# One keys' pass per chunk in the additive attention, and another order of work at the end of the last layer

## The chip, the cores and the metric

The kernel runs on one core of a Trainium2 chip. The core's engines are TensorE (PE in the profile; its weight loads stand apart as PEld), VectorE (DVE), ScalarE (ACT), GpSimd (POOL) and SyncE (SP). Here SP issues nearly all of the DMA transfers. Each engine works through its own queue in order, and waits on semaphores for the others. "granted clock" (PEclk) is the share of TensorE's full clock that it was granted in a stretch.

The metric is the device time of one execution in microseconds. The kernel before was run three times: 6970.31, 6976.12 and 6979.77, median 6976.12.

## The reference

Four layers work on four images (B = 4) of 56 x 56 tokens with 128 channels, in float32. Only layers 2 and 3 are touched. With `t` of shape (4, 3136, 128) they compute:

```python
# layer 2: additive attention (16 hidden units), then an expert layer
xn = layernorm(t)
f, g = xn @ W1[:128], xn @ W1[128:]                   # (4, 3136, 16): queries and keys
s = einsum('bija,a->bij', tanh(f[:, :, None] + g[:, None] + b1), w2) + b2
e = exp(s) * strictly_lower_triangle
t = t + (e / (e.sum(-1) + 1e-10)) @ xn
p = softmax(layernorm(t) @ gate_w.T, axis=tokens)     # 64 experts, each takes its 8 tokens
t = t + scatter(experts(gather(p)), p)                # 128 -> 512 -> 128, gelu
# layer 3: attention of the tokens on themselves, then a mixture of 8 experts
xn = layernorm(t)
t = t + softmax(xn @ xn.T) @ xn
xn = layernorm(t)
gate = two largest of softmax(xn @ router_w), divided by their sum
t = t + sum over e of gate[:, e] * (xn @ expert_w[e] + expert_b[e])
```

The `tanh` of layer 2 is the large term: for each pair of a query and an earlier key there are 16 of them.

## The kernel before, in words

All of `t` stays on the chip in `X[b]`, as 28 tiles of 112 tokens an image, each [112 tokens, 128 channels]. The time of the span goes to layer 0 until about 500, to layer 1 (a state-space scan) until about 2985, to layer 2 until about 5552 and to layer 3 until 6972.4.

**Layer 2's attention** (`layer2_attention`, L1139). An image has four chunks of seven query tiles (WT = 7, 784 queries), 16 chunks in all. A chunk goes over its key tiles J, from the image's first to the chunk's own last, and each key tile in two halves; (chunk, key tile, half) is a *piece*, and `pieces` lists all of them in order. One piece goes through five steps on three engines:

- `adds` (VectorE, L1298): seven operations that add one column of the keys' term `g` to the queries' term `fT` [128, up to 784], written into one of three rooms `th` of a ring;
- `tangents` (ScalarE, L1307): one Tanh over the whole room, in place;
- `scores` (TensorE, L1321): 28 small matmuls by `place`, which holds w2, into the bank `s`;
- `weights` (ScalarE, L1335): Exp once both halves are there; in the chunk's own key tiles GpSimd masks one square (L1342);
- `weighted` (TensorE, L1351): matmuls of `e` with the normalised tokens `xk` into `o`.

The piece loop issues, for piece i, in this order: the tanh of i, the *first slot* (`deal`), the adds of i + 2, at the first half of a key tile the `weighted` of an earlier key tile, the scores of i, what the first slot left for VectorE, the Exp of an earlier piece, and the *second slot* (`deal`). The order on each engine is the order of this text (a manual schedule). A slot takes one step from four lists: `urgent`, `now`, `later_on` (in every other slot) and `behind`. Narrow pieces, those at the diagonal, have fewer slots: a slot costs credit, which a piece gives in proportion to its width. A step may return a function, its VectorE part; the part of a first slot runs behind the scores of the same piece, that of a second slot at the start of the next slot. So a first slot's matmuls stand before the adds and scores, a second slot's behind them.

**A chunk's preparation** (`chunk_steps`, L1208) is such a list of steps, made for the first four tiles and then for the other three: `norm` twice (VectorE, two tiles each, into `xa`, L1222), `turn` (TensorE turns the tiles, L1231, VectorE copies the bank into `xT`, L1234), `by_group` (GpSimd sets the ones column at L1238, SP issues eight DMAs that carry `xa` to `xk` in another order of rows), `keys` (eight matmuls over 56 or 42 columns, L1254, then VectorE's add of `b1` into `g`, L1262) and `queries` (one matmul over 448 or 336 columns, L1272, then VectorE's copy into `fT`, L1276). That makes twelve steps. `xa` and `xT` each have one room, of four tiles, and the PSUM bank `m`, through which `turn`, `keys` and `queries` pass, is a single one too. The steps of an image's next chunk come at key tile 1 of the chunk before. Those of the next image's first chunk come at key tile 8 of the image's last one, through `later_on`, behind fifteen steps of statistics (`image_steps`) that end with a square root on ScalarE (`root`, by way of `rstd`, L175, with its scratch `li_ve` and `li_q`). When the loop comes to the first adds of a new chunk and steps are left in `now` or `later_on`, `add_ahead` runs all of them in one go, called the drain below. The first chunk of all has its own code (`first_chunk`, L1374).

What comes behind the attention of an image, the choice of 8 tokens for each of 64 experts (`choose_steps`, L1596), its experts and the scatter of their results (`experts2_steps`, scatter matmuls at L1822), are steps of `behind`. The choice has a second square root, by `rstd` with the scratch `ln_ve` and `ln_q`. Whatever is left in `behind` at the end of layer 2 runs there, but for the last 14 steps (`carried`), which are dealt into the first units of layer 3.

**Layer 3** has units (image, chunk of four tiles, key tile of 128): seven chunks (0 to 6) and 25 key tiles, `weights` (one matmul, one Exp) and `weighted` (one matmul) each. When a chunk's last `o` matmul (L2005) is behind it, its steps are dealt to the following units by their numbers: `copied` (VectorE and ScalarE copy `o` to `oT`, L1969 and L1970), `added` twice (L1539 to L1547), then `normed_chunk` (statistics, root, newton, norm, turn) and `token_choice` (L2147): router, `choose` (the gates, L2184 to L2194), `experts` and `store`. `experts(k)` takes one tile through two matmuls (four experts each, L2200, into two rooms `pe`) and eight operations of VectorE that multiply an expert's product by its gate and add it to X (L2205). These stand at

```python
    + [(21 + 2 * k, bind(experts, k)) for k in range(TC)] + [(21 + 2 * TC, store)]
```

that is, with the 4 that `experts_chunk` adds, at least 25 units behind the chunk's end. For the last two chunks of the last image there are no units left there, and their steps run one after the other in order of number.

Of the kernel before, what the change touches and what calls it, by code (L numbers as in the profile page):

```python
# [11 lines left out]
AF = mybir.ActivationFunctionType  # L12
# [126 lines left out]
class Hybrid:  # L139
# [35 lines left out]
    def rstd(self, pool, var, shape, eps, tag, bufs=None):  # L175

        nc = self.nc
        ve = self.t(pool, shape, tag + "_ve", bufs=bufs)
# [4 lines left out]
        q = self.t(pool, shape, tag + "_q", bufs=bufs)  # L183
# [955 lines left out]
    def layer2_attention(self):  # L1139
# [5 lines left out]
        with ExitStack() as ctx:  # L1145
# [62 lines left out]
            def chunk_steps(j):  # L1208
# [18 lines left out]
                def turn(at, w):  # L1227
                    r["xT"] = self.t(big, [P, CH], "xT")
                    ps = m()
                    for i in range(w):  # L1230
                        nc.tensor.transpose(  # L1231
                            ps[:, i * TP : (i + 1) * TP], r["xa"][:, i, :], self.ident[:TP, :TP]
                        )
                    return lambda: nc.vector.tensor_copy(r["xT"][:, : w * TP], ps[:, : w * TP])  # L1234
# [15 lines left out]
                def keys(at, w):  # L1250
                    ps = m()[:, : w * NG]
                    by_key = r["xT"][:, : w * TP].rearrange("p (g j) -> p g j", j=JG)
# [6 lines left out]
                    def keyed():  # L1259
                        if at == 0:  # L1260
                            g[b, k] = self.t(big, [P, WT * NG], f"g{k}")
                        nc.vector.tensor_scalar(  # L1262
                            g[b, k][:, at * NG : (at + w) * NG], ps, b1, None, op0=ALU.add
                        )
# [3 lines left out]
                def queries(at, w):  # L1268
                    if at == 0:
# [3 lines left out]
                        ps, wf.rearrange("p j a -> p (j a)"), r["xT"][:, : w * TP],  # L1273
# [4 lines left out]
                for at in range(0, n, TC):  # L1278
                    w = min(TC, n - at)
                    steps += [bind(norm, at, 0, 2), bind(norm, at, 2, w)]  # L1280
                    steps += [bind(f, at, w) for f in (turn, by_group, keys, queries)]
                return steps
# [91 lines left out]
            def first_chunk():  # L1374
# [5 lines left out]
                xT = [self.t(big, [P, CH], "xT"), self.t(sm, [P, WT * TP], "fT")]  # L1380
# [470 lines left out]
    def layer3(self):  # L1851
# [6 lines left out]
        with ExitStack() as ctx:  # L1858
# [103 lines left out]
            def experts_chunk(b, c):  # L1962
# [9 lines left out]
                def added(s):  # L1972
# [5 lines left out]
                    + [(k + 4, f) for k, f in self.token_choice(b, c, w, sm, m, ps_e)]  # L1978
# [168 lines left out]
    def token_choice(self, b, c, w, sm, m, ps_e):  # L2147
# [62 lines left out]
        def store():  # L2210
            dst = self.out[b].rearrange("h w c -> (h w) c").rearrange("(t p) c -> p t c", p=TP)
            nc.sync.dma_start(out=dst[:, TC * c : TC * (c + 1), :], in_=x4)

        bind = lambda f, *args: lambda: f(*args)
        return (
            self.normed_chunk(b, c, sm, m, w["eps"], turned, ones=True)
            + [(10, route), (12, exp), (13, choose)]
            + [(21 + 2 * k, bind(experts, k)) for k in range(TC)] + [(21 + 2 * TC, store)]
        )

# [47 lines left out]
```

## Time and profile before

| what | us |
|---|---|
| median of three runs | 6976.12 |
| the profiled execution: its time | 6974.18 |
| the profiled execution: its span | 6972.4 |
| mean granted clock of TensorE | 0.935 |
| busy in the span: PE / DVE / ACT / POOL | 6051.8 / 5757.1 / 4834.7 / 2787.6 |
| Tanh of layer 2 (L1307), 559 records | 2177.6, idle before it 138.4 |
| adds of layer 2 (L1298), 3920 records | 1864.2, idle before it 232.7 |
| scores of layer 2 (L1321), 14112 records | 1387.5 |
| experts of layer 3 on VectorE (L2205), 896 records | 311.8, idle before it 306.7 |

The profiled execution lies 1.94 below the median. In a row of the groups, the time after the bar is the busy time of the group and the mean duration of one in ns; after the second bar stands how long the engine stood still just before these instructions, and what ended most of that. A row of the waits reads "who waited <- for whom: us, times" and, where there is a third number, the longest. A row of the timeline has the start, the duration and the instruction, and in square brackets the wait ahead of it. A row of the windows has the stretch, its length, the busy time of PE, PEld, DVE, ACT and POOL with the number of instructions, the granted clock, and the DMA engines' share and rate.

### The profile page before, as it was taken

The numbers are of one execution on the slowest core, as the hardware profiler recorded it, in microseconds if no ns is written. First come the engines' busy times: TensorE is split into PE (matmuls) and PEld (weight loads), VectorE is DVE, ScalarE is ACT, GpSimd is POOL, SyncE is SP. The second block draws the span as 40 slices with busy tenths as digits, with TensorE's granted clock in tenths as the row PEclk, the third lists the DMA queues.
The fourth block names the chain that finished last, engine by engine and source line by source line (L and its number), as shares of the span: only waits on it lengthen the run. The fifth ranks groups of instructions, "written<-read, shape, count | busy, mean of one in ns | idle before, by whom it ended". The sixth has DMA issues, their size and how long they took to land.

```text
span 6972.4 us, 103013 instructions
## 1 busy us (share of the span) xinstructions
PE 6051.8 (87%) x37386; PEld 2623.8 (38%) x37386; DVE 5757.1 (83%) x10104; ACT 4834.7 (69%) x4839; POOL 2787.6 (40%) x1921
## 2 busy tenths in 40 slices
PE   8889989998999999877777877877788799999998
PEld 7633332333233333232233323332333355555554
DVE  6879999999999999988878888888897753566665
ACT  5567667766766677679999998999899833322231
POOL 2369989998999999910000000100101100000000
PEclk9989989998999899889998999999899999999999
DMA  3057767776777677700000000000003204343433
GB/s 53 5 138 189 184 162 186 186 182 169 187 184 179 174 187 184 178 9 3 1 6 3 8 2 6 4 6 3 6 20 123 83 21 149 78 108 89 119 86 95
DMA packets 363457, 654.29 MB, mean 94 GB/s; under 512 B 95412, under 2 KB 211908, under 8 KB 362437
## 3 DMA queue, kind: packets, MB, share of 16 engines
q1 hardware_dynamic: 362949, 647.71, 37.0%
q8 instruction: 296, 4.85, 0.3%
q14 instruction: 212, 1.74, 0.1%
HBM read 536.78 MB, written 104.37 MB: 92 GB/s over the span
## 4 chain that ended last, share of the span: by engine, by line
PE 23%; ACT 11%; DVE 11%; issue 10%; POOL 1%; SPq 1%; DMA 1%; DVEq 0%; ACTq 0%; POOLq 0%
ACT th L1307 9%; PE o L2005 6%; DVE th L1298 6%; PE q L1993 5%; PE s L1321 4%; PE pe L2200 2%; DVE X L2205 2%; ACT e L1335 1%; PE o L1351 1%; DVE wide L2025 1%; PE m L1254 1%; PE m L1539 1%; PE m L1822 0%; POOL e L1342 0%; DVE X L1547 0%
## 5 line engine op out<-in xcount | busy, mean ns | idle before, releaser
L1307 ACT ACTIVATE th<-th 128x5488 f32<-128x5488 f32 (+13 forms) x559 | 2177.6, 3944 | 138.4 <-DVE th L1298 124.2
L1298 DVE TENSOR_SCALAR th<-fT,g 128x784 f32<-128x784 f32 (+13 forms) x3920 | 1864.2, 548 | 232.7 <-PE s L1321 221.0
L1321 PE MATMUL s<-th,place 128*32 128x392 f32 (+5 forms) x14112 | 1387.5, 487 | 456.1 <-ACT th L1307 454.1
L860 DVE TENSOR_TENSOR_SCAN hs<-E,u 128x896 f32<-128x896 f32 x728 | 1449.1, 2006 | 3.9 <-ACT E L844 3.9
L844 ACT ACTIVATE E<-E,rate 128x448 f32<-128x448 f32 x1456 | 885.8, 661 | 127.2 <-DMA E<-delta_dram 124.3
L865 POOL TENSOR_TENSOR hs<-hs,room 128x896 f32<-128x896 f32 x448 | 925.5, 2087 | 82.6 <-DVE hs L860 82.2
L1321 PEld LDWEIGHTS s<-th,place 128*32 128x32 f32 (+1 forms) x14112 | 456.9, 112 | 1323.3 <-ACT th L1307 687.4
L865 POOL TENSOR_TENSOR hs<-hs,bc 128x896 f32<-128x896 f32 x448 | 927.3, 2090 | 46.7 <-DVE hs L860 44.1
L1998 ACT ACTIVATE e<-q,shift 128x448 f32<-128x448 f32 (+1 forms) x511 | 322.5, 634 | 669.3 <-PE q L1993 650.3
L1342 POOL TENSOR_TENSOR e<-e,later 112x112 f32<-112x112 f32 x112 | 102.3, 914 | 1178.3 <-ACT e L1335 670.8
L2205 DVE SCALAR_TENSOR_TENSOR X<-pe,r_gate,X 112x128 f32<-112x128 f32 x896 | 311.8, 348 | 306.7 <-PE pe L2200 271.1
L871 PE MATMUL y<-hs,sum 128*32 128x448 f32 x3584 | 499.4, 631 | 4.0 <-POOL hs L865 4.0
L1993 PE MATMUL q<-xT 128*128 128x448 f32 (+1 forms) x1022 | 499.5, 571 | 0.9 <-ACT e L1998 0.9
L2005 PE MATMUL o<-e,xk 128*128 128x448 f32 (+1 forms) x1022 | 477.6, 551 | 16.0 <-ACT oT L1970 16.0
L806 PE MATMUL u<-room,pick 32*128 32x448 f32 x1456 | 413.6, 638 | 68.5 <-DVE hs L860 66.6
L806 PE MATMUL u<-du,pick 32*128 32x448 f32 x1456 | 402.8, 618 | 74.3 <-DVE hs L860 72.9
L1351 PE MATMUL o<-e,xk 112*128 112x392 f32 (+5 forms) x1024 | 393.9, 505 | 34.6 <-POOL e L1342 31.5
L1238 POOL MEMSET xa<- 112x4 f32 (+1 forms) x30 | 55.0, 1832 | 919.6 <-PE m L1231 919.6
L853 DVE TENSOR_TENSOR u<-u,bc 128x896 f32<-128x896 f32 x364 | 391.8, 1077 | 25.9 <-PE u L806 25.7
L853 DVE TENSOR_TENSOR u<-u,room 128x896 f32<-128x896 f32 x364 | 391.7, 1076 | 22.0 <-PE u L806 21.9
L2134 POOL MEMSET lc_xa<- 112x4 f32 x28 | 3.1, 110 | 943.5 <-DVE lc_xa L2128 694.6
L848 ACT ACTIVATE u<-u 128x896 f32<-128x896 f32 x168 | 151.9, 904 | 296.9 <-PE u L797 217.2
(333 smaller groups left out, 8768.1 us busy)
## 6 DMA issues: line engine op xcount, KB each, us to landing
E<-delta_dram SPq DMA_DIRECT2D x728, 448.0 KB
V<-du_dram SPq DMA_DIRECT2D x168, 448.0 KB
wide<-in_L_ffn_weight SPq DMA_DIRECT2D x64, 1024.0 KB
r<-M SPq DMA_DIRECT2D x189, 224.0 KB
M<-wide SPq DMA_DIRECT2D x72, 392.0 KB
du_dram<-room SPq DMA_DIRECT2D x112, 112.0 KB
delta_dram<-room SPq DMA_DIRECT2D x112, 112.0 KB
du_dram<-du SPq DMA_DIRECT2D x112, 112.0 KB
```

What stands on the lines that cost most here:

```text
L806: nc.tensor.matmul(halves(to)[:, k], w["pick"][own, q, :], pre[j]["du"][own, f], start=True, stop=True,)
L844: nc.scalar.activation(e, e, AF.Exp, scale=rate)
L853: eng.tensor_mul(v, v, pre[p // PAIRS]["bc"][:, 0:1].to_broadcast([P, 2, CH]))
L860: nc.vector.tensor_tensor_scan(flat, E.pop(p), V.pop(p), 0.0, op0=ALU.mult, op1=ALU.add)
L865: nc.gpsimd.tensor_mul(HS[p], HS[p], bc[:, 1:2].to_broadcast([P, 2, CH]))
L871: nc.tensor.matmul(py[j, f][r * HD : (r + 1) * HD, :], w["sum"][:, q, :], HS[p + r // 2][:, r % 2], start=False, stop=(q == QG - 1),)
L1298: nc.vector.tensor_scalar(th[i][:, s, lo:hi], fT[j][:, lo:hi], g[b, J // WT][:, at : at + 1], None, op0=ALU.add,)
L1307: nc.scalar.activation(own, own, AF.Tanh)
L1321: nc.tensor.matmul(ps[j, J][QW * blk : QW * blk + rows, h, lo:hi], place[:, off : off + rows], z[:, at + s, h * HALF + lo : h * HALF + hi] ...
L1351: nc.tensor.matmul(po[j][:, h, lo:hi], xk[b, J // WT][:, J % WT, :], e[:, h * HALF + lo : h * HALF + hi], start=(J == 0), stop=(J == t + ( ...
L1993: nc.tensor.matmul(ps[:n, :CH], of_tile(xT[b], t), xT[b][:, c * CH : (c + 1) * CH], start=True, stop=True,)
L2005: nc.tensor.matmul(po[b, c], xk[b][:n, t, :], e[:n], start=first, stop=last)
```

## The change

In `chunk_steps`, `xT` holds seven tiles in place of four. Each `turn` writes its own part of it and `queries` reads its own part. `keys` is one step for the whole chunk, eight matmuls over 98 columns and one add, and stands before the last `queries`; the preparation has eleven steps. `first_chunk` takes its `xT` in the new size. The two square roots of layer 2 share the names, and so the rooms, of their scratch (`rt_ve`, `rt_q`).

In layer 3, the last chunk but one of the last image has its expert steps at 15, 16, 17 and 18. The last chunk has one step, `last_experts`: tiles 0 and 1 by `experts`, and between them tiles 2 and 3 another way. Their matmuls go into banks of `m` and of `q`, ScalarE multiplies the eight products of a tile by the gates into a room `y`, and VectorE sums the eight with one reduction and adds the sum to X. The chunk is stored in two halves.

```diff
@@ -175,12 +175,12 @@
     def rstd(self, pool, var, shape, eps, tag, bufs=None):
 
         nc = self.nc
-        ve = self.t(pool, shape, tag + "_ve", bufs=bufs)
+        ve = self.t(pool, shape, "rt_ve", bufs=bufs)
         nc.vector.tensor_scalar(ve, var, eps, None, op0=ALU.add)
         r = self.t(pool, shape, tag + "_r", bufs=bufs)
         nc.scalar.activation(r, ve, AF.Sqrt)
         nc.vector.reciprocal(r, r)
-        q = self.t(pool, shape, tag + "_q", bufs=bufs)
+        q = self.t(pool, shape, "rt_q", bufs=bufs)
         nc.vector.tensor_mul(q, r, r)
         nc.vector.tensor_mul(q, q, ve)
         nc.vector.tensor_scalar(q, q, -0.5, 1.5, op0=ALU.mult, op1=ALU.add)
@@ -1225,13 +1225,15 @@
                         )
 
                 def turn(at, w):
-                    r["xT"] = self.t(big, [P, CH], "xT")
+                    if at == 0:
+                        r["xT"] = self.t(big, [P, WT * TP], "xT")
+                    own = r["xT"][:, at * TP : (at + w) * TP]
                     ps = m()
                     for i in range(w):
                         nc.tensor.transpose(
                             ps[:, i * TP : (i + 1) * TP], r["xa"][:, i, :], self.ident[:TP, :TP]
                         )
-                    return lambda: nc.vector.tensor_copy(r["xT"][:, : w * TP], ps[:, : w * TP])
+                    return lambda: nc.vector.tensor_copy(own, ps[:, : w * TP])
 
 
                 def by_group(at, w):
@@ -1247,9 +1249,9 @@
                                 in_=r["xa"][of : of + rows, :w],
                             )
 
-                def keys(at, w):
-                    ps = m()[:, : w * NG]
-                    by_key = r["xT"][:, : w * TP].rearrange("p (g j) -> p g j", j=JG)
+                def keys():
+                    ps = m()[:, : n * NG]
+                    by_key = r["xT"][:, : n * TP].rearrange("p (g j) -> p g j", j=JG)
                     for i in range(JG):
                         nc.tensor.matmul(
                             ps, wg[:, P - AH - i * AH : 2 * P - AH - i * AH], by_key[:, :, i],
@@ -1257,11 +1259,8 @@
                         )
 
                     def keyed():
-                        if at == 0:
-                            g[b, k] = self.t(big, [P, WT * NG], f"g{k}")
-                        nc.vector.tensor_scalar(
-                            g[b, k][:, at * NG : (at + w) * NG], ps, b1, None, op0=ALU.add
-                        )
+                        g[b, k] = self.t(big, [P, WT * NG], f"g{k}")
+                        nc.vector.tensor_scalar(g[b, k][:, : n * NG], ps, b1, None, op0=ALU.add)
 
                     return keyed
 
@@ -1270,7 +1269,7 @@
                         fT[j] = self.t(sm, [P, WT * TP], "fT")
                     ps = m()[:, : w * TP]
                     nc.tensor.matmul(
-                        ps, wf.rearrange("p j a -> p (j a)"), r["xT"][:, : w * TP],
+                        ps, wf.rearrange("p j a -> p (j a)"), r["xT"][:, at * TP : (at + w) * TP],
                         start=True, stop=True,
                     )
                     return lambda: nc.vector.tensor_copy(fT[j][:, at * TP : (at + w) * TP], ps)
@@ -1278,8 +1277,8 @@
                 for at in range(0, n, TC):
                     w = min(TC, n - at)
                     steps += [bind(norm, at, 0, 2), bind(norm, at, 2, w)]
-                    steps += [bind(f, at, w) for f in (turn, by_group, keys, queries)]
-                return steps
+                    steps += [bind(f, at, w) for f in (turn, by_group, queries)]
+                return steps[:-1] + [keys, steps[-1]]
 
             def rounds(half):
 
@@ -1377,7 +1376,7 @@
                 r = im[0]
                 warm = self.t(wp, [P, 1], "warm")
                 nc.scalar.activation(warm, b1, AF.Tanh)
-                xT = [self.t(big, [P, CH], "xT"), self.t(sm, [P, WT * TP], "fT")]
+                xT = [self.t(big, [P, WT * TP], "xT"), self.t(sm, [P, WT * TP], "fT")]
                 fT[0] = self.t(sm, [P, WT * TP], "fT")
                 xk[0, 0] = self.t(big, [TP, WT, C], "xk0")
                 g[0, 0] = self.t(big, [P, WT * NG], "g0")
@@ -1975,7 +1974,7 @@
                 bind = lambda f, *args: lambda: f(*args)
                 return (
                     [(0, copied), (2, bind(added, 0)), (3, bind(added, 2))]
-                    + [(k + 4, f) for k, f in self.token_choice(b, c, w, sm, m, ps_e)]
+                    + [(k + 4, f) for k, f in self.token_choice(b, c, w, sm, m, ps_e, ps_q)]
                 )
 
             def fetch(b, c, t):
@@ -2144,7 +2143,7 @@
             (0, stats), (2, root), (3, newton), (4, norm), (7, turn), (8, lambda: turned(r["ps"]))
         ]
 
-    def token_choice(self, b, c, w, sm, m, ps_e):
+    def token_choice(self, b, c, w, sm, m, ps_e, ps_q):
 
         nc = self.nc
         tile4 = lambda tag, n: self.t(sm, [TP, TC, n], tag)
@@ -2207,16 +2206,48 @@
                         op0=ALU.mult, op1=ALU.add,
                     )
 
-        def store():
+        def store(k0=0, k1=TC):
             dst = self.out[b].rearrange("h w c -> (h w) c").rearrange("(t p) c -> p t c", p=TP)
-            nc.sync.dma_start(out=dst[:, TC * c : TC * (c + 1), :], in_=x4)
+            nc.sync.dma_start(out=dst[:, TC * c + k0 : TC * c + k1, :], in_=x4[:, k0:k1, :])
+
+        def last_experts():
+            half = TC // 2
+            room = self.t(self.f2_wide, [P, S], "wide")[:TP, : half * (E3 + 1) * C].rearrange(
+                "p (k e c) -> p k e c", k=half, e=E3 + 1
+            )
+            y, total = room[:, :, :E3], room[:, :, E3]
+            for k in range(half):
+                experts(k)
+                pes = []
+                for e0 in range(0, E3, 4):
+                    pe = (self.t(ps_q, [P, 512], "q") if k else m()).rearrange("p (e c) -> p e c", c=C)
+                    nc.tensor.matmul(
+                        pe[:TP].rearrange("p e c -> p (e c)"),
+                        r["xT"][:, (half + k) * TP : (half + k + 1) * TP],
+                        w["ew"][:, e0 : e0 + 4, :].rearrange("p e c -> p (e c)"), start=True, stop=True,
+                    )
+                    for e in range(4):
+                        nc.scalar.activation(
+                            y[:, k, e0 + e, :], pe[:TP, e, :], AF.Identity,
+                            scale=r["gate"][:, half + k, e0 + e : e0 + e + 1],
+                        )
+            store(0, half)
+            for k in range(half):
+                x = x4[:, half + k, :]
+                nc.vector.tensor_reduce(
+                    total[:, k], y[:, k].rearrange("p e c -> p c e"), axis=AX.X, op=ALU.add
+                )
+                nc.vector.tensor_add(x, total[:, k], x)
+            store(half, TC)
 
         bind = lambda f, *args: lambda: f(*args)
-        return (
-            self.normed_chunk(b, c, sm, m, w["eps"], turned, ones=True)
-            + [(10, route), (12, exp), (13, choose)]
-            + [(21 + 2 * k, bind(experts, k)) for k in range(TC)] + [(21 + 2 * TC, store)]
-        )
+        steps = self.normed_chunk(b, c, sm, m, w["eps"], turned, ones=True)
+        steps += [(10, route), (12, exp), (13, choose)]
+        if (b, c) == (B - 1, NCH - 1):
+            return steps + [(14, last_experts)]
+        first, stride = (15, 1) if (b, c) == (B - 1, NCH - 2) else (21, 2)
+        steps += [(first + stride * k, bind(experts, k)) for k in range(TC)]
+        return steps + [(first + stride * TC, store)]
 
 
 @with_exitstack
```

## The prediction

> **What bounds the kernel now.** All times are us from the span's start. I read the busy times by stage first, to see which engine each stage of the kernel leaves no room on.
>
> ```profile
> core 0: us, PE busy (x) PEld busy (x) DVE busy (x) ACT busy (x) POOL busy (x), PEclk, DMA share, GB/s
> 2985.00:5552.00 2567.00, 2001.75 (x17175) 813.31 (x17173) 2149.18 (x4980) 2412.69 (x995) 200.86 (x256) 0.94 0.06 19
> 5552.00:6930.00 1378.00, 1312.00 (x4503) 745.63 (x4504) 799.16 (x2869) 406.87 (x766) 31.79 (x195) 0.98 0.36 94
> 6930.00:6972.40 42.40, 24.69 (x54) 8.80 (x52) 29.25 (x108) 1.61 (x5) 0.21 (x2) 0.76 0.05 12
> ```
>
> Layer 2's attention (first row) is ScalarE's: 2412.69 of 2567 busy. Layer 3 is TensorE's (1312 of 1378). The last 42.4 us belong to no engine's throughput but to a chain, mostly VectorE's. The change touches the first and the last. So the second view is who waited for whom in layer 2.
>
> ```profile
> ACT th L1307 <- DVE th L1298: 124.2, 65, 8.9
> DVE fT L1276 <- PE m L1272: 63.8, 25, 6.4
> DVE g L1262 <- PE m L1254: 31.2, 13, 3.8
> DVE xa L1222 <- DMA xk<-xa: 1.8, 3, 0.7
> ```
>
> ACT idles 124 us for VectorE's adds; that is all that faster chunk steps can win. VectorE itself stands 63.8 us for the queries' matmul and 31.2 us for the keys'. It hardly waits for the transfers that empty `xa` (1.8). The timeline of the preparation of image 0's third chunk shows one case, and the windows the clock beside it.
>
> ```profile
> 3099.15 3.84 DVE L1298 TENSOR_SCALAR th<-fT,g 128x784 f32<-128x784 f32 x7
> 3099.28 2.00 PE L1254 MATMUL m<-xT,wg 128*128 128x42 f32 x16 [1.10 <-DVE xT L1234]
> 3101.09 2.14 PE L1351 MATMUL o<-e,xk 112*128 112x392 f32 x4
> 3103.17 3.89 PE L1321 MATMUL s<-th,place 128*32 128x392 f32 x28
> 3107.86 0.51 DVE L1276 COPY fT<-m 128x336 f32<-128x336 f32 x1 [4.70 <-PE m L1272]
> 3112.24 4.78 ACT L1307 ACTIVATE th<-th 128x5488 f32<-128x5488 f32 x1 [2.44 <-DVE th L1298]
> ...
> 3102.00:3104.00 2.00, 2.00 (x10) 0.44 (x13) 1.16 (x3) 2.00 (x1) 0.00 (x0) 0.50 0.10 25
> ```
>
> The keys wait 1.10 for `xT`, take 2.00, and the scores behind them run at a granted clock of 0.50 (3.89 instead of the usual 2.83). The queries come behind these scores, VectorE waits 4.70, its next adds are late and ACT idles 2.44. The same happens at 3229 (2.44), 3738 (5.71), 4380 (5.68) and 5022 (4.02). Last, the tail.
>
> ```profile
> 6930.49 1.88 PE L2200 MATMUL pe<-ew,f_xT 128*112 128x512 f32 x4
> 6931.55 3.12 DVE L2205 SCALAR_TENSOR_TENSOR X<-pe,r_gate,X 112x128 f32<-112x128 f32 x8 [7.91 <-PE pe L2200]
> 6934.59 0.38 DVE L1969 COPY oT<-o 128x224 f32<-128x224 f32 x1
> 6944.36 3.09 DVE L2205 SCALAR_TENSOR_TENSOR X<-pe,r_gate,X 112x128 f32<-112x128 f32 x8
> 6955.79 4.54 DVE L2205 SCALAR_TENSOR_TENSOR X<-pe,r_gate,X 112x128 f32<-112x128 f32 x12
> 6961.12 7.73 DVE L2205 SCALAR_TENSOR_TENSOR X<-pe,r_gate,X 112x128 f32<-112x128 f32 x20 [0.79 <-PE pe L2200]
> ```
>
> VectorE stands still 7.91 us although the gates of the last chunk but one are ready, then does that chunk's experts between the links of the last chunk's chain, and 32 more operations at the end.
>
> **Part by part.** The sum is made on the profiled execution, 6974.18 (span 6972.4); the median shown is 6976.12, 1.94 above.
>
> *A, the last chunk but one.* Its expert steps move from 21, 23, 25, 27 to 15 to 18, into the last chunk's units. TensorE comes to them at about 6924.5 instead of 6930.49, VectorE 1.06 later (as in the rows), at 6925.6. Four groups of 3.12 end at 6938.1. There are only two `pe` buffers, so pairs 2 to 4 wait on TensorE for VectorE (until 6928.9, 6932.0, 6935.1), and the last chunk's `o` matmuls queue behind: the last three (2.26) end at about 6938.3. So `oT` is copied at 6938.4 instead of 6934.59. From there: 1.9 to `den` (copy, ACT's half, matmul), 1.9 for two `added`, 1.6 for the statistics, 0.7 for ACT's root: newton at 6944.5 instead of 6947.37. Gain 2.8; bounds 1 (if the clock falls in those waits) and 7.9 (VectorE's whole wait).
>
> *B, the last chunk.* From newton to the first expert operation is 8.42 as before: 6953.0. Sixteen operations on VectorE take 6.2 (0.39 apart), with about 0.8 of waiting for a pair (as at 6961.12): 6960.0. ACT meanwhile makes 16 products of 112x128 from PSUM. No row shows one; between 0.20 (112x4) and 0.35 (128x224 copy), nearer the latter: 0.30, 4.8 in all, behind TensorE's pairs until about 6961. Then two reductions of 1024 elements by the row of 64x3136 (3.40, 1.085 ns an element): 1.2 each (bounds 1.1, and 2.4 if the stride doubles it), with adds of 0.2: 6962.9. Before it was 6968.85. The store is half as large; its end took 3.55, I take 3.4. Gain of A and B 6.0, so B is 3.2; bounds 0 (TensorE at half clock, 0.85 a matmul as at 6952.69, and slow reductions) and 5. One more issue on SP (0.34) lies beside the reductions.
>
> *C, fewer steps.* In the last image three steps fewer stand before the work dealt behind, and the instruction order shows two scatter steps (8 matmuls, 1.12 each step) moved from layer 3, which is TensorE's, into layer 2. Gain 2.2; bounds 0 and 2.2 plus their waits, 3.
>
> *D, keys once, where it gains.* Eight matmuls and one 0.26 add go per chunk, 15 times. One pass of 98 columns: bounds 2.00 (42 columns, so it is not the columns that cost) and 4.0; I take 2.1. More important: one step fewer changes the parity of the slots. Queries now come in the slot before the adds, keys in the slot behind the scores. By hand, from 3084: no long wait of VectorE, and its adds end at 3108.9, before ACT needs them (3110.2). What is left of 0.44 + 2.44 is 0.8. Likewise 2.1 at 3229, 4.2 at 3738 and 4380, 2.5 at 5022: 15.1 in all at full clock. If the clock falls there as in the row of 0.50 (TensorE stands 1.4 to 1.9 between keys and queries, for `g` now comes behind VectorE's adds and the single `m` bank holds the queries back), 4.5 is left. I take the middle, 9.8.
>
> *E, F, G, a new wait.* The second half's `norm` needs the only `xa` back from eight transfers, which land 7.7 after their first issue (3642.60 to 3650.33). Two steps stood between, now one. VectorE waits, and the adds queued behind it. Where pieces are wide there is slack: 0.4 each in three preparations, 1.2 (G). In the narrow ones not: in image 0's first chunk `norm` is wanted at 3019.2 and `xa` free at 3023.65; the chain moves by 2.0 (E). Before each second chunk of images 1 to 3 it is wanted at 3647.0 and free at 3650.3; a third of it comes through to the gap of 8.89 behind the drain: 1.1 each, 3.3 (F). Bounds 0 and 3.3 each.
>
> *H, the root.* In three images ACT's Sqrt stands one tanh earlier, and must wait for adds that it did not wait for: 0 to 2.2 each, I take 1.0: 3.0.
>
> Shared names for the root's scratch and the wider `xT` add no instruction; the two users of the scratch lie 238 us apart (3506.9 and 3744.7), so no wait. Stores and tables are as many as before.
>
> Sum: -2.8 -3.2 -2.2 -9.8 +2.0 +3.3 +1.2 +3.0 = -8.5: 6965.7 for the profiled execution, 6967 as a median.
>
> On the clock, the Trainium skill ("TensorE: Matmul & The Clock Gate", Part 1) says that the clock halves only behind an idle window of about 3.4 us. The trace differs: it halves at 3102 though TensorE stood still for 1.10 at most. By that rule nothing in D would be slowed, D would be 15.1 and the sum 6960; by the row it can be.
>
> **The rivals.** *Keys win all.* The clock holds, since 98 columns keep TensorE busier than 42, and the new waits stay hidden: D 15.1, E to H together 3: 6974.2 - 8.2 - 15.1 + 3 = 6954, 6956 as a median. For it: the first keys of 56 columns, without a wait ahead, keep 1.00. Against: the wait for `xa` is seen already, 0.63 and 0.75. *Layer 2 unmoved.* ACT is 94% busy there, and D is eaten by E to H: only A to C, 6966, 6968 as a median; it can't be told from the forecast. *Slower: the transfers of `xa`.* If VectorE has no slack anywhere, each of 15 preparations loses up to 3.3, 49 in all, against 18 won: about 7005. It decides from 2.1 lost in each ((18 + 14) / 15). For it: VectorE is 84% busy in layer 2, the wait lies in front of the adds. Against: 15 long waits of VectorE go at the same time, and three preparations (at 3526, 4170, 4812) take one step a piece and have time.
>
> **How the numbers follow.** About 0.2%, 14 us, is what a measurement of this kernel tells from no change. Forecast 0.33, layer 2 unmoved 0.18, keys win all 0.32, slower 0.17. The forecast and layer 2 unmoved are within 0.2%: 0.51. With all terms at their best bounds the median is 6949, at their worst 6984. The range leaves out the slower rival and a few hundredths at the low end: 6950 to 6986.
>
> **What would show it.** A: the last `oT` copy at 3 to 4 us later against the last gates, behind 32 operations without a break. B: 16 ACT products, end of the span about 11 us behind the last gates' first use. D: the waits of `fT` for `m` fall from 63.8 below 20, and no ACT gap of over 2 near the third and fourth chunks. E to G: `xa` waits for its transfers 20 us or more in all. Wrong if the clock falls in more places, if the reductions with a stride cost over 2, or if ACT's idle time for adds in layer 2 grows over 140.

## The result, and the profile after

Over 11 runs each, the changed kernel took 6957.97 (6953.23 to 6962.66) and the kernel before 6975.91 (6968.69 to 6979.77): a ratio of 0.9976, 95% interval 0.9967 to 0.9986. It is 17.9 faster by the medians. The profiled execution after took 6962.66, its span is 6960.8, so the two profiles differ by 11.6 only. What lies ahead of layer 2, work that the change does not touch, happened to be 2.4 longer after: the first tanh of layer 2 starts at 3002.03 before and at 3004.42 after. In the twelve profiles of this study it starts between 2994.79 and 3004.42, so single runs of this kernel differ by some 10 us before the change begins to act. What follows is therefore counted inside layer 2 and layer 3, from the start of one tanh to that of another.

The busy times by stage of the kernel after, with the stages cut at the same work as before:

```profile
core 0: us, PE busy (x) PEld busy (x) DVE busy (x) ACT busy (x) POOL busy (x), PEclk, DMA share, GB/s
2985.00:5546.50 2561.50, 1969.01 (x16951) 796.42 (x16951) 2149.74 (x4975) 2410.64 (x996) 179.63 (x256) 0.95 0.06 19
5546.50:6918.40 1371.90, 1304.92 (x4474) 742.13 (x4475) 797.81 (x2867) 406.30 (x765) 31.76 (x195) 0.98 0.36 95
6918.40:6960.80 42.40, 26.76 (x68) 11.13 (x66) 28.54 (x96) 6.60 (x22) 0.21 (x2) 0.85 0.05 11
```

ScalarE has the same work in layer 2 (2410.64 busy) in a shorter stretch; TensorE has some 33 less. The waits in layer 2 after (who waited, for whom, us, times, longest):

```profile
ACT th L1306 <- DVE th L1297: 113.8, 61, 9.8
DVE g L1263 <- PE m L1256: 30.4, 13, 4.7
DVE xa L1222 <- DMA xk<-xa: 30.1, 12, 3.6
DVE fT L1275 <- PE m L1271: 11.9, 6, 2.4
```

ScalarE's wait for the adds fell by 10.4 only, though VectorE's wait for the queries fell from 63.8 to 11.9. Two waits took their place. VectorE now waits 30.1 for the transfers that empty `xa` (1.8 before). And ScalarE waits for the root's input where it hardly did (2.6 in three images before):

```profile
ACT ln_r L181 <- DVE rt_ve L179: 15.7, 3, 5.3
```

The preparation of image 0's third chunk after, with the clock beside it; the last rows are windows at, or just behind, the keys' pass of the five preparations in which the prediction had seen a gap:

```profile
3102.15 3.11 PE L1256 MATMUL m<-xT,wg 128*128 128x98 f32 x16
3105.55 0.32 DVE L1263 TENSOR_SCALAR g<-m,b 128x98 f32<-128x98 f32 x1
3105.93 0.83 PE L1271 MATMUL m<-xT,wf 128*128 128x336 f32 x2 [0.66 <-DVE g L1263]
3106.59 1.48 PE L1350 MATMUL o<-e,xk 112*128 112x392 f32 x4
3108.01 2.84 PE L1320 MATMUL s<-th,place 128*32 128x392 f32 x28
3109.54 0.51 DVE L1275 COPY fT<-m 128x336 f32<-128x336 f32 x1
3111.70 9.44 ACT L1306 ACTIVATE th<-th 128x5488 f32<-128x5488 f32 x2
...
3101.00:3105.00 4.00, 4.00 (x28) 3.03 (x22) 4.00 (x8) 3.45 (x1) 0.50 (x1) 1.00 0.10 25
3217.00:3221.00 4.00, 3.97 (x25) 2.91 (x19) 3.15 (x6) 4.00 (x2) 0.00 (x0) 1.00 0.16 37
3721.00:3725.00 4.00, 3.59 (x23) 2.88 (x17) 3.65 (x8) 4.00 (x2) 0.00 (x0) 1.00 0.15 34
4363.00:4367.00 4.00, 3.62 (x25) 1.70 (x28) 3.99 (x8) 4.00 (x2) 0.00 (x0) 1.00 0.06 12
5002.00:5006.00 4.00, 3.59 (x19) 2.23 (x21) 3.46 (x8) 4.00 (x2) 0.00 (x0) 1.00 0.11 25
```

The keys' pass of 98 columns takes 3.11 at a granted clock of 1.00 (the prediction took 2.1, from its reading that the columns do not cost), and the queries stand before the adds: no wait in front of the copy to `fT`, none in front of ScalarE's tanh. The end:

```profile
6918.69 1.88 PE L2199 MATMUL pe<-ew,f_xT 128*112 128x512 f32 x4
6919.75 3.12 DVE L2204 SCALAR_TENSOR_TENSOR X<-pe,r_gate,X 112x128 f32<-112x128 f32 x8 [1.70 <-PE pe L2199]
6923.31 6.16 DVE L2204 SCALAR_TENSOR_TENSOR X<-pe,r_gate,X 112x128 f32<-112x128 f32 x16 [0.44 <-PE pe L2199]
6929.69 3.12 DVE L2204 SCALAR_TENSOR_TENSOR X<-pe,r_gate,X 112x128 f32<-112x128 f32 x8 [0.22 <-PE pe L2199]
6932.99 0.39 DVE L1968 COPY oT<-o 128x224 f32<-128x224 f32 x1 [0.18 <-PE o L2004]
6946.72 3.12 DVE L2204 SCALAR_TENSOR_TENSOR X<-pe,r_gate,X 112x128 f32<-112x128 f32 x8
6950.22 3.13 DVE L2204 SCALAR_TENSOR_TENSOR X<-pe,r_gate,X 112x128 f32<-112x128 f32 x8 [0.37 <-PE pe L2199]
6951.97 2.18 ACT L2230 ACTIVATE wide<-q,r_gate 112x128 f32<-112x128 f32 x8 [1.29 <-PE q L2224]
6953.30 1.88 DVE L2237 TENSOR_REDUCE wide<-wide 112x128 f32<-112x1024 f32 x1
6955.42 1.87 DVE L2237 TENSOR_REDUCE wide<-wide 112x128 f32<-112x1024 f32 x1
```

VectorE's 7.91 in front of the experts are down to 1.70, and its last 32 operations became 16 and two reductions of 1.88.

Layer 2 is ScalarE's, so the starts of its tanh (L1307 before, L1306 after) are a clock on which each stretch can be read. The table adds up, for the changed kernel (after) and the ten kernels of the experiments (e1 to e10), how much longer or shorter than before a stretch became (us, from the timelines; chunks are counted from 0 to 15, four to an image; a chunk goes from the start of its first tanh to that of the next chunk's).

| stretch | after | e1 | e2 | e3 | e4 | e5 | e6 | e7 | e8 | e9 | e10 |
|---|---|---|---|---|---|---|---|---|---|---|---|
| chunk 0 | +3.2 | 0.0 | +3.2 | +0.8 | -0.5 | 0.0 | +3.2 | +3.2 | 0.0 | +0.1 | -0.5 |
| chunks 1 and 2 | -3.8 | 0.0 | -4.0 | +1.2 | -4.5 | -5.8 | -3.6 | -3.7 | 0.0 | -5.8 | -4.5 |
| chunks 4, 8, 12, with the drains | +7.1 | +0.7 | +6.6 | +5.0 | -3.0 | -3.9 | +6.1 | +6.9 | +0.8 | -4.5 | -1.8 |
| chunks 5, 9, 13, with the root | -1.6 | -3.9 | -1.6 | -6.0 | -3.5 | -0.6 | -13.1 | -1.2 | +13.9 | -14.0 | -14.6 |
| chunks 6, 10, 14 | -15.0 | +4.3 | -15.7 | +2.5 | -15.8 | -17.2 | -15.8 | -15.7 | +2.7 | -17.2 | -15.5 |
| chunks 3, 7, 11 | 0.0 | -0.1 | +1.5 | +1.7 | 0.0 | 0.0 | +1.7 | +0.1 | 0.0 | +0.1 | 0.0 |
| chunk 15 | +2.3 | -0.4 | +2.0 | -2.1 | +2.3 | +2.4 | +2.9 | +2.4 | +3.1 | +2.7 | +5.0 |
| layer 2 | -7.9 | +0.5 | -7.9 | +3.1 | -25.0 | -25.0 | -18.6 | -7.9 | +20.6 | -38.8 | -31.9 |

Kernels with the same layer 2 show how far a row can be trusted. e2 and e7 have that of the changed kernel and lie within 1.5 of it in every row. e1 has that of the kernel before: it lies within 0.7 of it in five rows, but is 3.9 shorter at chunks 5, 9 and 13 and 4.3 longer at chunks 6, 10 and 14. The sums agree to 0.5. So a row is good to some 4 us, and the last line to about one.

### The profile page after: what moved, and what is told of

Same layout as the page of the kernel before. It is cut to its first block, busy times and chain, and to the rows that moved or that the text cites. A ratio compares the mean times of both kernels' runs of the same rounds, so it can differ in the third digit from the quotient of the medians.

```text
span 6960.8 us, 102439 instructions
## 1 busy us (share of the span) xinstructions
PE 6015.7 (86%) x37146; PEld 2606.4 (37%) x37146; DVE 5754.4 (83%) x10077; ACT 4837.2 (69%) x4855; POOL 2764.6 (40%) x1921
## 4 chain that ended last, share of the span: by engine, by line
PE 21%; ACT 14%; DVE 11%; issue 10%; SPq 1%; POOL 1%; DMA 1%; DVEq 0%; ACTq 0%; POOLq 0%
ACT th L1306 11%; PE o L2004 6%; DVE th L1297 6%; PE q L1992 5%; PE s L1320 4%; PE pe L2199 2%; DVE X L2204 2%; ACT e L1334 1%; PE o L1350 1%; DVE wide L2024 1%; PE m L1538 0%; SPq L1247 0%; PE m L1821 0%; PE m L1256 0%; DVE X L1546 0%
## 5 line engine op out<-in xcount | busy, mean ns | idle before, releaser
L1306 ACT ACTIVATE th<-th 128x5488 f32<-128x5488 f32 (+13 forms) x559 | 2177.7, 3944 | 122.2 <-DVE th L1297 113.8
L1320 PE MATMUL s<-th,place 128*32 128x392 f32 (+5 forms) x14112 | 1371.1, 483 | 497.8 <-ACT th L1306 495.9
L1341 POOL TENSOR_TENSOR e<-e,later 112x112 f32<-112x112 f32 x112 | 80.3, 717 | 1237.2 <-ACT e L1334 709.5
```

What stands on the lines that cost most here:

```text
L1306: nc.scalar.activation(own, own, AF.Tanh)
L1320: nc.tensor.matmul(ps[j, J][QW * blk : QW * blk + rows, h, lo:hi], place[:, off : off + rows], z[:, at + s, h * HALF + lo : h * HALF + hi] ...
```

## The experiments

**Each half of the change alone.** e1 has only the new functions of layer 3, e2 only the changed `chunk_steps`, `first_chunk` and `rstd`; the rest is the kernel before. The kernel before was run again beside each group of experiments. Its median was 6975.91 beside the change, 6970.82 beside e1 to e4, 6971.39 beside e5 to e7 and 6971.28 beside e8 to e10, so each run is read against its own.

```diff
 # e1: in token_choice and its call as in the change; layer 2 as before
 # e2: in chunk_steps, first_chunk and rstd as in the change; layer 3 as before
```

> Only layer 3's end is changed, layer 2 is as before. From the two traces, the stretch from the gates of the last chunk but one to the end went from 48.8 to 42.8, and the rest of layer 3 took as long as before. If the parts are independent: 6.0 under the kernel before, ratio 0.9991, and no gain in the first image of layer 3. If the shorter end needs the other arrangement of layer 2 (the scatter steps that left layer 3): less than 3 under before.

> Only layer 2 is changed, the end of layer 3 is as before. By the chain of tanh in the two traces layer 2 gained 7.9; by the medians of the whole change (17.9) less the 6.0 of the end it would be 12. Independent parts: 8 to 12 under before, ratio 0.9983 to 0.9989, the last tanh 8 earlier against the first.

Measured: e1 6962.72 beside 6970.82 before, ratio 0.9991 (0.9982 to 1.0000); e2 6958.48, ratio 0.9984 (0.9975 to 0.9992). By medians the parts are 8.1 and 12.3, 20.4 together, against 17.9 for the whole: as independent parts would be, as far as these runs can tell (the interval of e1 alone reaches 1.0000). Layer 2 of e2 is 7.9 shorter by its chain, as in the whole.

**Slots or less work.** The change does two things to a preparation: it takes away eight matmuls and an add, and it makes the list one step shorter, so that each later step changes from a slot before the scores to one behind them, or the other way. e3 keeps the first and undoes the second; e4 does the second without the first.

```diff
 # e3, in the changed kernel
-                    steps += [bind(f, at, w) for f in (turn, by_group, queries)]
-                return steps[:-1] + [keys, steps[-1]]
+                    steps += [bind(f, at, w) for f in (turn, by_group)]
+                    steps += [keys if at else lambda: None, bind(queries, at, w)]
+                return steps
 # e4, in the kernel before
-                    steps += [bind(norm, at, 0, 2), bind(norm, at, 2, w)]
+                    steps += [bind(norm, at, 0, 2), bind(norm, at, 2, w)] if at == 0 else [bind(norm, at, 0, w)]
```

> The changed kernel with an empty step where the first keys stood: twelve steps again, so every later step of a chunk and of the choice stands in the slot in which it stood before; still eight matmuls and one add fewer in each chunk, and xa has its old time. Theory 'slots' (layer 2's gains come from the shift by one slot): the gaps of ScalarE at the third and fourth chunks are back, layer 2 gains 0 to 3, the kernel is 6 to 9 under before. Theory 'less work' (they come from the matmuls that are gone): layer 2 keeps its gains without the losses of xa and the root, about 18, the kernel 24 under before.

> The kernel before, with the two norm steps of a chunk's second half made one: eleven steps, the keys twice as before, as many matmuls and adds as before, layer 3 as before. Later steps stand one slot earlier, as in the changed kernel, and xa keeps two steps for its transfers. Theory 'slots': layer 2 gains the 18 that the changed kernel shows beside its losses at the drains and the first chunk (10.3), so 12 to 18 under before. Theory 'less work': 0 to 2 under before, or slower.

Measured: e3 6977.09, ratio 1.0012 (1.0003 to 1.0021), slower than before although its end of layer 3 is the short one; e4 6946.39, ratio 0.9964 (0.9951 to 0.9976), 24.4 faster although it makes the keys twice and has no shorter end. The waits of e3 first (ScalarE's for the adds, VectorE's for the queries' matmul and for `xa`), then those of e4 (ScalarE's for the adds, VectorE's for the queries, and the root's for its input):

```profile
ACT th L1307 <- DVE th L1298: 132.4, 69, 10.6
DVE fT L1275 <- PE m L1271: 55.0, 17, 4.5
DVE xa L1222 <- DMA xk<-xa: 23.1, 12, 3.0
```

```profile
ACT th L1307 <- DVE th L1298: 98.1, 58, 7.6
DVE fT L1276 <- PE m L1272: 21.3, 14, 1.9
ACT ln_r L181 <- DVE ln_ve L179: 13.9, 3, 4.6
```

So layer 2's gain is in the main the slots' and not the matmuls'. With the old slots and eight matmuls fewer, the wait for the queries stays (55.0) and layer 2 is 3.1 longer; with the new slots and all matmuls, it is 25.0 shorter, more than the 12 to 18 that was expected. Its column in the table has the -15.8 at chunks 6, 10 and 14 that the changed kernel has, and e3 has +2.5 there. One thing in e3's expectation was wrong: `xa` did not get its old time. The empty step gives back the slot, but not the time. VectorE waits 23.1 for the transfers, 0.8 of it in the first chunk, 5.0 in the three drains, where steps run back to back, and the rest in the slots of wide pieces; that it comes there earlier because it has no first keys to wait for is likely, but not shown. The first chunk is 0.8 and the drains are 5.0 longer. Without these losses layer 2 of e3 would be some 3 shorter than before, so the matmuls that were saved may be worth a few microseconds, but not the 25.0 of e4. One thing stays open in e3. In its trace layer 2 is 3.1 longer, the stretch from the last tanh to the 1381st `o` matmul of layer 3 is 3.6 longer (nine stretches of half clock where before has seven), and the end is 6.5 shorter, so it is as fast as before from the first tanh on; but the traced execution (6971.26) is the fastest of its eleven, and their median is 6.3 slower than before.

**The room of `xa`.** In the changed kernel, the second half's tiles go into the room of `oT`, free at that time.

```diff
-                        r["xa"] = self.t(big, [TP, TC, C], "xa")
+                        r["xa"] = self.t(big, [TP, TC, C], "xa") if at == 0 else self.t(
+                            sm, [P, WT * TP], "oT", bufs=1
+                        )[:TP, : TC * C].rearrange("p (k c) -> p k c", c=C)
```

> The changed kernel with the second half's normalised tiles in the room of oT, which is free then, in place of the single xa: its norm waits for no transfer. Against the first tanh, the chain of tanh of the changed kernel lost 3.2 in the first chunk and 1.5, 3.3 and 2.2 at the drains ahead of images 1 to 3. Theory 'xa' (these are the waits for the eight transfers): all 10 come back, 10 under the changed kernel, the waits of xa for its transfers fall from 30.1 to under 3. Rival (the drain is longer because the keys' pass of 98 columns and the last queries now stand in it together): at most 3 come back, though the waits for transfers go.

Measured: 6938.93, ratio 0.9951 (0.9936 to 0.9965), 32.5 under the kernel before, where the changed kernel was 17.9 under it; by the table, layer 2 is 17.1 shorter than the changed kernel's. The wait for transfers is gone; what is left at this line is

```profile
DVE xa L1224 <- issue: 0.7, 3, 0.2
```

The first chunk gave back all 3.2 and the drains 11.0 (from +7.1 to -3.9). The rival allowed 3. That is more than the 10 expected, because the drains became shorter than before by 3.9, and chunks 1 and 2 gave 2.0 more. Why the drains gave back more than was lost in them is not shown.

**The root's slot.** `rooted` stood in slot 8 of the choice's list, with slots 7 and 9 empty. e6 moves it to 9 in the changed kernel, e8 to 7 in the kernel before; nothing else moves.

```diff
-            (0, 1, [bind(stats, t) for t in range(0, NT, 4)]), (8, 1, [rooted]),
+            (0, 1, [bind(stats, t) for t in range(0, NT, 4)]), (9, 1, [rooted]),   # e6; 7 in e8
```

> The changed kernel with the root of the choice one slot later (9 instead of 8; slot 9 was empty, nothing else moves), so it stands behind one more tanh on ScalarE. In the changed kernel ScalarE waits 5.1 to 7.5 there for VectorE's statistics. Theory 'root': in that wait a tanh that is ready is run, 3 to 4.5 in each of three images, 9 to 13 under the changed kernel, and the wait of ln_r falls from 23.2 to under 8. Rival (the adds are late anyway, and the wait goes over to the tanh): within 3 of the changed kernel.

> The kernel before with the root of the choice one slot earlier (7 instead of 8, an empty slot), nothing else: step H of the prediction alone. The prediction gave it 1.0 in each of three images, 3.0. Against the changed kernel the run with the later root showed 4.0 in each. Theory 'the root costs 4 wherever it stands ahead of the tanh': 12 over the kernel before. Rival (before, ScalarE waits there for adds in any case, so the two waits overlap): 3 or less over it.

Measured: e6 6947.21, ratio 0.9962 (0.9947 to 0.9977), 24.2 under the kernel before, 6 more than the changed kernel, with layer 2 10.7 shorter than there; e8 6989.63, ratio 1.0026 (1.0015 to 1.0036), 18 over the kernel before. The intervals of e6 and of the changed kernel overlap, so the table and the trace decide. (The 7.5 in e6's expectation is a wait at 2982, before the first tanh, not of the choice; the three of the choice are 5.3 at most.) ScalarE in image 1's choice, first in the changed kernel, then in e6, then in e8:

```profile
3730.24 4.78 ACT L1306 ACTIVATE th<-th 128x5488 f32<-128x5488 f32 x1
3735.04 1.28 ACT L181 ACT_TABLE_LOAD   x1
3741.45 0.23 ACT L181 ACTIVATE ln_r<-rt_ve 112x28 f32<-112x28 f32 x1 [5.13 <-DVE rt_ve L179]
3742.99 4.78 ACT L1306 ACTIVATE th<-th 128x5488 f32<-128x5488 f32 x1
```

```profile
3733.41 4.78 ACT L1306 ACTIVATE th<-th 128x5488 f32<-128x5488 f32 x1 [1.05 <-DVE th L1297]
3738.21 1.28 ACT L181 ACT_TABLE_LOAD   x1
3739.50 0.23 ACT L181 ACTIVATE ln_r<-rt_ve 112x28 f32<-112x28 f32 x1
3741.85 4.77 ACT L1306 ACTIVATE th<-th 128x5488 f32<-128x5488 f32 x1
```

```profile
3734.32 1.28 ACT L181 ACT_TABLE_LOAD   x1
3746.93 0.23 ACT L181 ACTIVATE ln_r<-ln_ve 112x28 f32<-112x28 f32 x1 [11.32 <-DVE ln_ve L179]
```

With one tanh more ahead of it the root waits for nothing, and the tanh runs in what was its wait. At chunks 5, 9 and 13 this is worth 11.5 on the changed kernel (from -1.6 to -13.1). One slot earlier in the kernel before it costs 13.9 there. Both are near the 12 of the theory, and the rival's 3 is out. All of layer 2 is 20.6 longer in e8; the other 6.7 lie in rows that moved by 3.1 at most, and are not explained.

**The stride of the reduction.** ScalarE's eight products for one output element are put side by side.

```diff
-                            y[:, k, e0 + e, :], pe[:TP, e, :], AF.Identity,
+                            y[:, k, :, e0 + e], pe[:TP, e, :], AF.Identity,
-                    total[:, k], y[:, k].rearrange("p e c -> p c e"), axis=AX.X, op=ALU.add
+                    total[:, k], y[:, k], axis=AX.X, op=ALU.add
```

> The changed kernel with the eight products of an output element side by side in the room that ScalarE writes and VectorE sums, so the reduction reads without a stride and the 16 products are written with one. If the stride makes the reduction slow (1.88 instead of the 1.2 from the contiguous row of 64x3136): 1.2 each, the end 1.4 earlier, ScalarE's products as long as before (0.27). If a reduction's time goes by its outputs and not by its stride: 1.88 as before. If the strided writing costs: more than 0.4 a product, and the end no earlier. The whole time moves by less than its uncertainty in each case; the trace decides.

Measured: 6956.71, ratio 0.9977 (0.9968 to 0.9987), not to be told from the changed kernel. The trace decides:

```profile
6948.21 2.30 ACT L2231 ACTIVATE wide<-q,r_gate 112x128 f32<-112x128 f32 x8 [1.22 <-PE q L2225]
6949.48 1.22 DVE L2238 TENSOR_REDUCE wide<-wide 112x128 f32<-112x1024 f32 x1
6950.95 1.21 DVE L2238 TENSOR_REDUCE wide<-wide 112x128 f32<-112x1024 f32 x1
```

The reduction takes 1.22 instead of 1.88: it was the stride. Eight products written with a stride take 2.30 instead of 2.18. On the path that is some 1.3.

**Together.** e9 is the changed kernel with e5, e6 and e7; e10 is e4 with the changed end of layer 3, e6 and e7, that is with the keys twice.

```diff
 # e9: changed kernel + second xa in oT's room + (9, 1, [rooted]) + rows together
 # e10: kernel before + merged norm + the changed end of layer 3 + (9, 1, [rooted]) + rows together
```

> The changed kernel with the second half's tiles in oT's room, the root one slot later and the reduction's rows together. If the three gains add up on the changed kernel: 17.1 + 10.7 + 1.4, about 6929 beside a kernel before of 6971 (ratio 0.994). If the gains of the first two share a slack of ScalarE: 6936 to 6940.

> The keys twice, norm merged, the changed end of layer 3, the root one slot later and the rows together. By the single runs: 6946 less 6 for the end, 8 to 12 for the root and 1.4: about 6928. If the keys' pass made once is worth anything beside the slots, the run before this one is the faster of the two; by 'slots' they are within 4 of each other.

Measured: e9 6927.94 beside 6971.28, ratio 0.9936 (0.9923 to 0.9950); e10 6931.41, ratio 0.9942 (0.9929 to 0.9954). e9 is 43.3 and e10 39.9 under the kernel before, against 17.9 for the changed kernel. The gains add up: layer 2 of e9 is 38.8 shorter than before. In e9, ScalarE's wait for the adds in layer 2 is down to

```profile
ACT th L1308 <- DVE th L1299: 99.3, 56, 8.5
```

and its root no longer appears among the waits. The 3.5 between e9 and e10 lies within their intervals, so by the medians making the keys once, with the slots the same, is worth nothing that these runs can show. The two traces differ by more, 38.8 and 31.9 in layer 2, so a few microseconds for the keys made once are not ruled out; e5 and e4, the same pair with the old root slot, are equal there (25.0).

## Why the prediction was right, and where it was not

The range (6950 to 6986) holds 6957.97. The point was 6967 (the sum as printed gives 6967.6), 9 too high, and the likeliest case, no change within 0.2%, was narrowly missed by the middle value: the kernel is 0.24% faster (0.14 to 0.33). Neither of the likely cases happened as told. The time is next to that of "keys win all" (6956), whose gain in D came about in full, but its condition that the new waits stay hidden did not hold: E, F and H cost 21.8, where the forecast had 8.3. What made up for them, 15.0 at chunks 6, 10 and 14, was not in the sum at all. That the time fell well inside the range is therefore in good part luck: the direction and the two halves of the mechanism were right, most sizes were not, and the errors cancelled.

- **A, B (the end of layer 3): right.** From the gates of the last chunk but one to its successor's newton the traces have 23.7 before and 20.2 after, 3.5 (forecast 2.8). From the first expert operation of the last chunk to the end of the span it is 16.6 and 14.1, 2.5 (forecast 3.2): the reductions took 1.88 instead of 1.2, 1.4 more on the path. Together 6.0, as forecast; e1 has 8.1 by medians.
- **C (two scatter steps leave layer 3): 0.3 instead of 2.2.** 16 matmuls went, 104 in place of 120 in layer 3. But from the last tanh to the 1381st of the 1400 `o` matmuls it takes 1372.7 before and 1372.4 after. In e2, with the same steps moved, it is 1370.5; that trace has six stretches of half clock between 5590 and 6920, where before and after have seven. Over the twelve traces the length of this part goes by their number and not by the kernel: 1370.5 and 1370.6 with six, 1372.4 to 1373.2 with seven (eight traces, three of them with 120 scatter matmuls and five with 104), 1374.2 with eight, 1376.4 with nine. The gain was there at first: the 51st `o` matmul comes 90.3 behind the last tanh before and 87.8 after. At the 351st, still in the first image, 0.5 of it is left (471.7 and 471.2). What swallowed the rest was not tested.
- **D (the five gaps): mis-sized, 9.8 instead of 16.9.** In image 0 it brought 3.8. In the chunks 5, 9 and 13 the sum with the root is -1.6, and e6 shows that the root costs 11.5 of it, so D is 13.1 there. (Read against e1, whose layer 2 is also the old one, that is 9.2, and D 13.0.) The mechanism was the one told (the queries before the adds), and e3 and e4 show that it is mostly this and not the matmuls: with the old slots, e3 has nothing of it at chunks 1 and 2 (+1.2), and at chunks 5, 9 and 13, where its root stands as before, 6.0, or 2.1 against e1. What failed is the middle between the two clocks: at the keys' pass of the five preparations (3101, 3217, 3721, 4363 and 5002) the windows show a clock of 1.00 throughout. D at full clock had been put at 15.1. The rule of the Trainium skill ("TensorE: Matmul & The Clock Gate", Part 1), that the clock halves behind an idle window of about 3.4 us, gave that end and a sum of 6960. The outcome in D agrees with it, but the clock of 0.50 that the kernel before showed from 3101.9, where TensorE had stood still for 1.10 at most, still speaks against its condition.
- **E (first chunk): mis-sized, 2.0 instead of 3.2.** All of it was the wait for `xa` (e5).
- **F (the drains): mis-sized, 3.3 instead of 7.1.** The wait was seen, but only a third of it was let through. The three waits for `xa` there are 2.60, 3.18 and 2.70 (at 3651, 4290 and 4929), and nearly all of that came through; e5 gets back 11.0.
- **G: not to be told from 1.2.** The prediction does not say which three preparations it means. Those in chunks 3, 7 and 11 have no wait for `xa` and took as long as before; in the wide pieces of chunks 1, 2, 6, 10 and 14 e5 gets back 4.2 in all, within what a row can be trusted.
- **H (the root one tanh earlier): mis-sized, 3.0 instead of 11.5.** It was priced at 0 to 2.2 in each image. The root itself waits for the last statistics, 5.13 in image 1, with its table loaded, and a tanh that is ready or nearly so stands behind it.
- **Not in the sum: -15.0 at chunks 6, 10 and 14, and +2.3 in chunk 15.** The prediction followed the slots of the five preparations with a long gap only, and in images 1 to 3 these are the third chunks'. But the step that went shifts everything behind it, also the `added` steps and the long steps of the choice (a 3.4 match-and-replace). Which of them brought how much was not taken apart. An example is ScalarE's wait at 4478 before, 3.79 for `den` behind a matmul that stood behind the scores:

```profile
4474.66 2.83 PE L1321 MATMUL s<-th,place 128*32 128x392 f32 x28
4477.81 0.15 DVE L1543 TENSOR_SCALAR den<-m 112x1 f32<-112x1 f32 x1
4478.01 4.78 ACT L1307 ACTIVATE th<-th 128x5488 f32<-128x5488 f32 x1 [3.79 <-DVE den L1543]
```

The same wait is 1.00 in images 1 and 3; the long one stands close behind a stretch of half clock (6.83 from 4463.9). After, the tanh of that piece runs without a wait. That it is the shift is shown by e4, which has it without the change (-15.8), and by e3, which has the change without it (+2.5; e1, with the old layer 2, has +4.3).

The rival on the other side, slower by the transfers of `xa`, was right in its mechanism and wrong in its reach: the wait grew to 30.1 and took all of its 10.3 in the narrow pieces and the drains; in the wide ones (chunks 1, 2, 6, 10 and 14) e5 gets back 4.2 in all, far from 3.3 in each of 15 preparations.

Of what the prediction said would show, the 16 products, the order of the 32 operations and the `xa` wait of 20 or more came; the waits of `fT` fell below 20; the last `oT` copy came at 6932.99, 14.9 behind the gates, where before it was 11.0, so 4 later against them. The five gaps of ScalarE in front of a tanh are gone, but not every gap of over 2 near the third and fourth chunks: their first tanh still waits 2.9 to 3.2, and the root's waits of 5.1 to 5.3 are new. The end of the span came 14.1 behind the first use of the last gates and not 11; the prediction's own sum gives 13.3 there. None of its signs of being wrong came: the mean clock is 0.938 (0.935 before), the reductions took 1.88, ScalarE's wait for adds 113.8. The bounds of the terms, as printed, add up to 6945 and 6987 and not to 6949 and 6984.

## What to carry to other kernels

Where steps are dealt into slots by their place in a list, taking one step out changes the place of all that follow; count what that does to every step behind it before pricing the work that was saved, and test the two apart, by an empty step in place of the one taken out and by joining two steps of the old list. A wait on an engine that is the bound costs what could have run in it: put a step whose input is late behind work that is ready. A transfer that was hidden by a step in between shows up when that step goes; another room for the data got all of it back.

## What the runs showed of the hardware

- A reduction of eight terms to 112x128 took 1.88 when the terms lay 128 elements apart, and 1.22 when they lay side by side. The ScalarE products that write them took 2.18 for eight when written in a row and 2.30 with a stride of eight elements; a single one is recorded with 0.36 to 0.41 and 0.47 to 0.52, and they overlap. The stride costs half as much again on the reading side and 5% on the writing side.
- The granted clock in the records of before and after halves for stretches that are multiples of 3.41 us (3.41, 6.83, 10.24 and so on). In layer 3, where TensorE is the bound, one of 3.41 should cost half of it, 1.7 by this estimate; between the traces above with six and with nine of them lie 5.8, 1.9 each. A gain of 2 there can be gone, or doubled, by one of them. One such stretch after:

```profile
6183.00:6187.00 4.00, 4.00 (x7) 1.52 (x7) 3.01 (x7) 0.63 (x1) 0.00 (x0) 0.57 0.92 185
6187.00:6191.00 4.00, 4.00 (x20) 2.31 (x18) 0.93 (x3) 1.54 (x3) 0.00 (x0) 1.00 0.94 205
```

- At a granted clock of 1.00, the 16 matmul records of a keys' pass took 3.11 with 98 columns (0.36 a record), 2.02 with 56 (at 3084 before) and 2.00 with 42 (at 3099 before). The time of these short matmuls is neither the same for all nor in proportion to the columns.
